# Layer 0: sampling-matrix matmuls issued two groups at a time, window products spread out, and the shared convolution block computed by ScalarE and GpSimd

## The chip, the cores and the metric

The kernel runs on one core of one Trainium2 chip. The metric is device microseconds of one execution of the program. The kernel before was run three times: 3473.86, 3480.29 and 3483.97 us, median 3480.29 us. One more execution was profiled; it took 3483.37 us, of which its trace spans 3481.5 us.

## The reference

Two layers act on x of shape (2, 512, 64, 64), float32. The change touches only layer 0, a deformable convolution with a residual; layer 1 (attention over the pixels, batch norm, residual) takes its result.

```python
# layer 0
x = x + L0(gn(x))                               # gn: group norm, 32 groups
# L0, with C=512, G=16 groups, 9 points, 64x64 pixels:
xproj  = inp @ in_w + in_b                      # 512x512 projection per pixel
x1     = depthwise_conv3x3(x) + dw_b            # 9 taps per channel
x1     = gelu(layernorm(x1) * ln_g + ln_b)
offset = x1 @ off_w + off_b                     # 16*9*2 columns
mask   = softmax((x1 @ mask_w + mask_b) by group)   # 16*9 columns
out    = sum over 9 points of mask * bilinear(xproj at point + offset)
out    = out @ out_w + out_b
```

## The kernel before

A period of layer 0 handles one chunk: 8 rows of 64 pixels, 512 pixels (`CH`), of one image. There are `NSEQ` = 16 chunks, 8 for each of two images. Channels lie in 4 blocks of 128 partitions (`KB`). Offsets are small enough that every sample falls into a 5x5 window around its pixel, so the bilinear gather is turned into a product: for each pixel and group, 25 window weights `aw`, then a matmul of those weights with patches of `xproj`.

Each chunk passes through generators, and every `yield` is a place at which another generator may go on:

- `project(i)`: normalizes the input (`xn`, ScalarE, L782), multiplies by `in_w` (`pq`, L792), copies (`xj`, L798) and stores to DRAM.
- `features(i)`: the depthwise convolution. One tap starts `conv` (L828 on ScalarE for the first three chunks, L830 on GpSimd after that), the other 8 taps in each of 4 blocks are multiply-adds on VectorE (L841), 32 in all. Then the mean over channels (`p_mean`, a matmul with ones, L855), the subtraction (L860), squares (L863), the variance, its root (L872), a reciprocal (L874), a product (L875) and Gelu (L879) into `feat`. For chunks 0 and 1, which fill the pipeline, GpSimd computes one block (`SHARED`) alone in `share`: a product (L821) and an addition (L822) for each of 8 taps.
- `weights(i)`: four tiles of 128 pixels, each four matmuls into `po` (L896) and an addition of the bias into `o` on VectorE (L903); exponent (L910), softmax, ramps `tx`, then nine products on VectorE (L941), of which eight are added into `aw` by GpSimd (L946). Products alternate between two buffers, `o[:, 0]` and `o[:, 1]`. The result is copied in four parts (`at`, ScalarE, L951), transposed by TensorE (`p_tr`, L960) and copied into `awT` (L961).
- `sample(i)`: eight groups of four matmuls `pb` (L989) spread the weights over the patch positions, each group copied by ScalarE into `bt` (L994); then eight groups of eight matmuls `pa` (L1008) with the patches, copied into `dT` (L1019), then four tiles of output `py` (L1028), each followed on VectorE by an addition into `res` (L1033) and statistics (L1034), and a store. `pb` and `pa` share two PSUM buffers (tag `big`); `po`, `py`, `pq`, `p_mean` and `p_tr` share four (tag `mm`).

A `pb` group reads `awT` on partitions `32*t` upward, with `t = c // 2`, c the column of the pixel in its strip of eight. So a group with d0 divisible by 8 uses t = 0 and 1, and the next one t = 2 and 3:

```python
for d0 in range(0, PR * PC, 4):
    for k in (0, 2, 1, 3):
        r, c = divmod(d0 + k, PC)
        off, t = SEL0 - (r * SX + c), c // 2
```

No scheduler reorders anything: `manual_schedule` keeps each engine's instructions in the order in which they are emitted, and `period` (L1058) writes out by hand how seven generators are interleaved: `y` is the sample of the chunk before (its last part), `v` the weights of this chunk, `m` its sample, `w` the weights of the next, `f` the features of the chunk after that, `g` those of a later one, `p` a projection, `more` statistics of the second image. `period` runs for chunks 0 to 13; `next_to_last` and `last_period` for 14 and 15. Before it, L1186 on fills the pipeline. A tile comes free when the last reader of its buffer is done, so a buffer's reuse is a wait on another engine.

Of the kernel before, what the change touches and what calls it, by code (L numbers as in the profile page):

```python
# [10 lines left out]
F32 = mybir.dt.float32  # L11
I32 = mybir.dt.int32
AF = mybir.ActivationFunctionType
ALU = mybir.AluOpType
# [562 lines left out]
def window_path(ctx: ExitStack, tc: tile.TileContext, t_in: dict, out: bass.AP, far: bass.AP, sums: bass.AP):  # L577
# [67 lines left out]
    with ExitStack() as l0:  # L645
# [159 lines left out]
        def features(i):  # L805
# [9 lines left out]
            def share(kb):  # L815

                x = io.tile([P, ROWS + 2, W], F32, name="raw", bufs=3)
                for tap in (0, 2, 3, 4, 5, 6, 7, 8):
                    dst, src, wt = tap_of(kb, tap)
                    part = x[:, :ROWS, : dst.shape[2]]  # L820
                    nc.gpsimd.tensor_scalar(part, src, wt, None, ALU.mult)  # L821
                    nc.gpsimd.tensor_add(dst, dst, part)  # L822

            fill = i < 2
            for kb in BLOCKS if i < 3 else range(KB):
                dst, src, wt = tap_of(kb, 1)
                if i < 3:
                    nc.scalar.activation(dst, src, AF.Identity, bias=dw_b[:, kb : kb + 1], scale=wt)  # L828
                else:
                    nc.gpsimd.tensor_scalar(dst, src, wt, dw_b[:, kb : kb + 1], ALU.mult, ALU.add)  # L830
                if fill and kb == SHARED:
                    share(kb)
                if fill or kb == KB - 1:
                    yield
            tot = None if fill else sm.tile([P, CH], F32, tag="tot", name="tot")
            for kb in BLOCKS if fill else range(KB):
# [23 lines left out]
            nc.vector.tensor_sub(a, a, mu.unsqueeze(1).to_broadcast([P, KB, CH]))  # L860
            f = cv.tile([P, KB, CH], F32, tag="feat", name="feat")
            for kb in range(KB):
# [10 lines left out]
            yield  # L873
            nc.vector.reciprocal(rstd, rstd)  # L874
            nc.vector.tensor_mul(a, a, rstd.unsqueeze(1).to_broadcast([P, KB, CH]))  # L875
            yield

# [9 lines left out]
        def weights(i):  # L887
# [5 lines left out]
            for t in range(4):  # L893
                po = ps.tile([P, CH], F32, tag="mm", name="po")
                for kb in range(KB):
                    nc.tensor.matmul(  # L896
                        po[:, : 3 * GP], f[:, kb, t * P : (t + 1) * P], om_w[:, kb].rearrange("p a k g -> p (a k g)"),
                        start=(kb == 0), stop=(kb == KB - 1),
                    )
                    if kb == 1:  # L900
                        yield
                yield
                nc.vector.tensor_add(  # L903
                    o[:, :, :, t * G : (t + 1) * G].rearrange("p a k g -> p (a k) g"),
                    po[:, : 3 * GP].rearrange("p (a g) -> p a g", g=G), om_b.rearrange("p a k g -> p (a k) g"),
                )
                yield
# [29 lines left out]
            for e, k in enumerate((4, 0, 1, 2, 3, 5, 6, 7, 8)):  # L937
                kx, ky = divmod(k, 3)
                dst = aw[:, ky : ky + 3, kx : kx + 3, :]
                pk = dst if k == 4 else o[:, e % 2].rearrange("p (y x) q -> p y x q", x=3)  # L940
                nc.vector.tensor_mul(  # L941
# [115 lines left out]
        def period(y, v, m, w, f, g, p, more, last, ahead, taps):  # L1057
# [12 lines left out]
            for k, count in enumerate(taps):  # L1070
                for _ in range(2):
                    m()
                    w()
                f(count)
                w()
                if k < 2:
                    more()
# [16 lines left out]
            y(2)  # L1094
            more()
            f()
            y()
            m()
            p()
            for k, steps in enumerate((2, 2, 1, 0)):  # L1100
                p()
                w(steps)
                if k == 0:
# [4 lines left out]
                if k == 2:  # L1108
                    more()
                    w(2)  # L1110
                if k < 3 and (k or not last):
                    m()
                if k == 0:
                    f()
                if k == 2:
                    w(2)
                    g()

        def next_to_last(y, v, m, w):

            v(4)
            y()
            w(12)
            for steps, tiles in ((1, 2), (1, 2), (2, 2), (1, 1)):
# [58 lines left out]
        def more():  # L1183
            next(later, None)

        with tc.manual_schedule():  # L1186
# [25 lines left out]
            p1(4)  # L1212
            f0(3)
            f1(8)
# [3 lines left out]
            p2()  # L1218
            v(3)
            f1()  # L1220
            for _ in range(3):
                more()
            p2(4)
            v(3)
            f()
            v(3)
            f(3)
            v(3)
            f1()
            f(3)  # L1230
            f1()
            v(2)
            p2(2)
            v(3)
            p2(2)
            v(4)
            f1()
            p2(2)
            v(5)
            f1(2)  # L1240
            p2(2)
            more()
            next(products)
            run(output_bias())
            more()
            f(4)
            v(4)
            for i in range(NSEQ):
# [7 lines left out]
                if i + 2 >= NSEQ:  # L1256
                    (next_to_last if i + 1 < NSEQ else last_period)(y, v, m, w)
                    y, v = m, w
                    continue
                ahead, taps = (4, (9, 7, 6, 6)) if i else (0, (4, 6, 6, 6))  # L1260
                period(y, v, m, w, f, g, Chain(project, i + 3), more, i + 3 == NSEQ, ahead, taps)
# [652 lines left out]
```

## Time and profile before

| what | value |
|---|---|
| median of three executions | 3480.29 us |
| the profiled execution | 3483.37 us |
| its span | 3481.5 us |
| layer 0, to the last `py` | about 1290 us |
| a period between 326 and 1144 us | 73.0 to 76.2 us, mean 74.4 |
| TensorE busy, 326 to 1144 us | 772.30 of 818 us |
| VectorE busy, same stretch | 640.54 us |
| ScalarE busy, same stretch | 569.11 us |
| GpSimd busy, same stretch | 345.56 us |
| mean granted TensorE clock | 0.969 |

The trace of one execution names each instruction's start, its length, and what ended the idle time before it. "x16" behind a matmul counts passes: a float32 matmul appears as two, a transpose as one. Busy time of TensorE includes pipelined ends, so a stretch of back-to-back matmuls is read from start to start. "Clock" is the share of full speed that TensorE was granted; it is 1.00 or 0.50 in any moment. Idle time of an engine off the chain costs nothing.

A period's start is taken here as the start of L860, once per period on VectorE: for example 626.88, 701.97 and 777.06 us.

### The profile page before, as it was taken

What the parts mean: (1) busy time and instruction counts of PE and PEld (TensorE: products, weight loads), DVE (VectorE), ACT (ScalarE), POOL (GpSimd) and SP (SyncE); (2) the same over time, 40 slices, a digit from 0 to 9 for tenths busy, and PEclk for the clock granted to TensorE, in tenths of its full rate; (3) what the DMA queues carried; (4) which work ended last, traced back from release to release, by engine and by line L of the source; (5) the groups of instructions that cost most, each with busy time, mean ns of one, the idle gap of its engine ahead of it and who ended that gap; (6) DMA issues with size and microseconds to landing.
All of it is one profiled execution on the core that took longest, in us unless ns stands there. A gap on an engine that the chain in (4) does not pass through costs nothing.

```text
span 3481.5 us, 38488 instructions
## 1 busy us (share of the span) xinstructions
PE 3227.7 (93%) x14171; PEld 2279.8 (65%) x14171; DVE 2666.6 (77%) x3682; ACT 1323.0 (38%) x1799; POOL 751.9 (22%) x674
## 2 busy tenths in 40 slices
PE   5889999999999789899999999999899999999990
PEld 2455555555555467578787787887578787787880
DVE  8788777778778648787696886977787696885875
ACT  2576766667767543211312203113221212202105
POOL 5344443344443310100101001000100101101112
PEclk9999999999999899999999999999999999999995
DMA  6334433223342248966768658656966767758788
GB/s 220 96 99 135 127 121 101 88 88 115 105 127 80 70 136 289 290 188 176 216 186 229 195 169 223 211 180 220 280 195 179 212 194 219 206 162 231 234 294 351
DMA packets 238390, 629.99 MB, mean 181 GB/s; under 512 B 28112, under 2 KB 45136, under 8 KB 237168
## 3 DMA queue, kind: packets, MB, share of 16 engines
q1 hardware_dynamic: 181456, 431.07, 37.9%
q0 software_dynamic: 43936, 159.40, 17.7%
q10 hardware_dynamic: 12800, 36.97, 3.0%
q8 instruction: 114, 1.87, 0.2%
q14 instruction: 84, 0.69, 0.1%
HBM read 410.15 MB, written 124.91 MB: 154 GB/s over the span
## 4 chain that ended last, share of the span: by engine, by line
PE 69%; DVE 14%; POOL 5%; DMA 4%; ACT 4%; issue 3%; SPq 0%; ACTq 0%; POOLq 0%; DVEq 0%
PE accy L1528 22%; PE accx L1528 17%; PE pS L1435 7%; PE py L1028 4%; POOL aw L946 4%; PE po L896 4%; PE pvy L1686 3%; DVE conv L841 3%; PE pb L989 2%; PE pa L1008 2%; PE pvx L1686 2%; PE pq L792 2%; PE pk L1758 1%; DMA wv<-vsum 1%; ACT at L951 1%
## 5 line engine op out<-in xcount | busy, mean ns | idle before, releaser
L1528 PE MATMUL accy<-tt,v 128*128 128x256 f32 x2016 | 601.0, 380 | 0.8 <-DVE ct L1557 0.6
L1440 ACT ACTIVATE e<-pS 128x1024 f32<-128x1024 f32 x256 | 248.3, 1021 | 723.4 <-PE pS L1435 719.2
L1528 PE MATMUL accx<-e,v 128*128 128x256 f32 x1792 | 472.8, 386 | 0.0
L1528 PE MATMUL accy<-e,v 128*128 128x256 f32 x1792 | 461.2, 380 | 0.0
L841 DVE SCALAR_TENSOR_TENSOR conv<-xn,L_conv_dw_w_sb,conv 128x504 f32<-128x504 f32 x496 | 420.5, 855 | 52.3 <-POOL conv L830 37.2
L1528 PEld LDWEIGHTS accy<-tt,v 128*128 128x128 f32 x2016 | 383.3, 190 | 54.9 <-DVE ct L1557 1.0
L1528 PEld LDWEIGHTS accx<-e,v 128*128 128x128 f32 x1792 | 334.6, 191 | 121.8 <-issue 80.7
L1528 PEld LDWEIGHTS accy<-e,v 128*128 128x128 f32 x1792 | 341.2, 190 | 46.6
L1507 DVE TENSOR_TENSOR tt<-e 128x256 f32<-128x256 f32 x448 | 187.8, 419 | 177.2 <-PE accy L1528 148.9
L1508 DVE TENSOR_TENSOR tt<-tt,e 128x512 f32<-128x512 f32 x448 | 310.0, 692 | 15.3
L1528 PE MATMUL accx<-tt,v 128*128 128x256 f32 x1008 | 300.9, 380 | 9.0 <-DVE tt L1507 9.0
L994 ACT COPY bt<-pb 96x1024 f32<-96x1024 f32 x124 | 243.9, 1975 | 162.3 <-PE pb L989 160.8
L1008 PEld LDWEIGHTS pa<-bt,patch 96*128 96x128 f32 x2048 | 247.7, 195 | 61.3 <-issue 31.4
L1435 PE MATMUL pS<-q,keys 64*128 64x512 f32 x1024 | 256.7, 620 | 9.2 <-ACT e L1440 9.2
L1008 PE MATMUL pa<-bt,patch 96*128 96x128 f32 x2048 | 251.9, 279 | 11.7 <-ACT bt L994 11.3
L946 POOL TENSOR_TENSOR aw<-aw,o 128x576 f32<-128x576 f32 x128 | 230.9, 1804 | 121.8 <-DVE o L941 114.2
L1028 PE MATMUL py<-dT,L_conv_out_w_sb 128*128 128x512 f32 x512 | 252.3, 640 | 1.4 <-ACT awT L961 1.4
L1449 POOL DMA_DIRECT2D tot<-e x144 | 124.0, 887 | 588.8 <-DVE e L1425 316.7
L792 PE MATMUL pq<-in_w,xn 128*128 128x512 f32 x512 | 235.1, 602 | 3.6 <-ACT xn L782 3.3
L1453 POOL DMA_DIRECT2D tot<-e x32 | 17.4, 544 | 974.0 <-DVE e L1425 835.8
L1533 ACT COPY u<-accx 128x256 f32<-128x256 f32 x56 | 20.8, 372 | 519.7 <-PE accx L1528 516.9
L896 PE MATMUL po<-om_w_pg,feat 128*128 128x432 f32 x512 | 217.0, 550 | 0.7 <-ACT feat L879 0.7
(245 smaller groups left out, 4721.8 us busy)
## 6 DMA issues: line engine op xcount, KB each, us to landing
v<-wv SPq DMA_DIRECT2D x436, 448.0 KB
tot<-e POOLq DMA_DIRECT2D x176, 512.0 KB, 7.0
patch<-xt SPq DMA_DIRECT2D x256, 192.0 KB
v<-ww SPq DMA_DIRECT2D x56, 448.0 KB
wv<-vform SPq DMA_DIRECT2D x48, 512.0 KB
wv<-vsum SPq DMA_DIRECT2D x48, 384.0 KB
xt<-xj SPq DMA_DIRECT2D x128, 128.0 KB
res<-in_x SPq DMA_DIRECT2D x64, 256.0 KB
```

What stands on the lines that cost most here:

```text
L792: nc.tensor.matmul(pq, xn[:, kb, 1 + 2 * t : 3 + 2 * t, :].rearrange("p r c -> p (r c)"), in_w[:, kb, :], start=(kb == 0), stop=(kb == KB ...
L841: nc.vector.scalar_tensor_tensor(dst, src, wt, dst, ALU.mult, ALU.add)
L896: nc.tensor.matmul(po[:, : 3 * GP], f[:, kb, t * P : (t + 1) * P], om_w[:, kb].rearrange("p a k g -> p (a k g)"), start=(kb == 0), stop=(k ...
L946: nc.gpsimd.tensor_add(dst, dst, pk)
L994: copy(bt[:SN].rearrange("s g q d -> s d (g q)")[:, d0 : d0 + 4, :], pb[:SN])
L1008: nc.tensor.matmul(pa[:, p], xp[:SN, p, cb * P : (cb + 1) * P], bt[:SN, 4 * cb : 4 * cb + 4, PX * s + p, :], start=True, stop=True,)
L1028: nc.tensor.matmul(py, out_w[:, kb, cb * P : (cb + 1) * P], dT[:, kb, :], start=(kb == 0), stop=(kb == KB - 1))
L1435: nc.tensor.matmul(p[:, a, :], keys[r, i, (2 * u + h) * P : (2 * u + h + 1) * P], c.q[r, qh, :], start=True, stop=True,)
L1440: nc.scalar.activation(e.rearrange("p a q -> p (a q)"), p.rearrange("p a q -> p (a q)"), AF.Exp)
L1507: nc.vector.tensor_sub(t[:, 0], x[:, 1], x[:, 3])
L1508: nc.vector.tensor_add(t[:, 1:3], t[:, 0].unsqueeze(1).to_broadcast([P, 2, HQ]), x[:, 0:3:2])
L1528: nc.tensor.matmul(out, v[:, blk, :], op, start=(first and g == 0), stop=(final and g == NG))
```

## The change

`share` puts its products on ScalarE, in two alternating buffers, and keeps the additions on GpSimd; it is emitted after all four first taps. Chunk 1 uses `awT` for its squares. In `weights`, the yield inside a tile's four matmuls is gone, and products use three buffers, `o[:, 2]` being free by then. A yield stands between the reciprocal and the product in `features`. In `period`, two steps of `m` now stand together, followed by one step of `w`, so two `pb` groups and then one whole `po` tile are emitted; 14 taps instead of 4 (8 instead of none in the first period) come ahead of the first output tile, 18 instead of 28 after it; and products stand around the reciprocal and its product. The order of the fill is rewritten.

```diff
             def share(kb):
-                x = io.tile([P, ROWS + 2, W], F32, name="raw", bufs=3)
-                for tap in (0, 2, 3, 4, 5, 6, 7, 8):
+                x = [io.tile([P, ROWS + 2, W], F32, name="raw", bufs=3) for _ in range(2)]
+                for k, tap in enumerate((0, 2, 3, 4, 5, 6, 7, 8)):
                     dst, src, wt = tap_of(kb, tap)
-                    part = x[:, :ROWS, : dst.shape[2]]
-                    nc.gpsimd.tensor_scalar(part, src, wt, None, ALU.mult)
+                    part = x[k % 2][:, :ROWS, : dst.shape[2]]
+                    nc.scalar.activation(part, src, AF.Identity, scale=wt)
                     nc.gpsimd.tensor_add(dst, dst, part)
...
-                if fill and kb == SHARED:
-                    share(kb)
                 if fill or kb == KB - 1:
                     yield
+            if fill:
+                share(SHARED)
...
-            f = cv.tile([P, KB, CH], F32, tag="feat", name="feat")
+            f = awT.rearrange("p g w -> p (g w)").rearrange("p (k c) -> p k c", k=KB)
+            if i != 1:
+                f = cv.tile([P, KB, CH], F32, tag="feat", name="feat")
...
             nc.vector.reciprocal(rstd, rstd)
+            yield
             nc.vector.tensor_mul(a, a, rstd.unsqueeze(1).to_broadcast([P, KB, CH]))
+            if i == 1:
+                f = cv.tile([P, KB, CH], F32, tag="feat", name="feat")
...
-                    if kb == 1:
-                        yield
                 yield
...
-                pk = dst if k == 4 else o[:, e % 2].rearrange("p (y x) q -> p y x q", x=3)
+                pk = dst if k == 4 else o[:, e % 3].rearrange("p (y x) q -> p y x q", x=3)
...
             for k, count in enumerate(taps):
-                for _ in range(2):
-                    m()
-                    w()
+                m(2)
+                w()
                 f(count)
                 w()
...
             more()
+            w(2)
             f()
+            w()
+            f()
+            w(2)
             y()
             m()
             p()
-            for k, steps in enumerate((2, 2, 1, 0)):
+            for k in range(4):
                 p()
-                w(steps)
...
                 if k == 2:
                     more()
-                    w(2)
+                    w()
                 if k < 3 and (k or not last):
                     m()
                 if k == 0:
                     f()
+                if k == 1:
+                    w()
...
             v(4)
             y()
-            w(12)
+            w(8)
...
-            f0(3)
+            f0(4)
             f1(8)
             next(products)
             fetch(0, 0)
             fetch(0, 1)
             p2()
-            v(3)
-            f1()
+            v(4)
             for _ in range(3):
                 more()
+            f1()
+            v(2)
+            f1()
+            v(2)
             p2(4)
-            v(3)
+            v()
+            f1()
+            v()
             f()
             v(3)
...
-                ahead, taps = (4, (9, 7, 6, 6)) if i else (0, (4, 6, 6, 6))
+                ahead, taps = (14, (5, 5, 4, 4)) if i else (8, (5, 5, 4, 4))
```

The rest of the rewritten fill only redistributes the same steps `v`, `f1`, `p2` and `f`. On TensorE the order of a period changes in one place: eight times "four `pb`, two `po`" becomes four times "eight `pb`, four `po`".

More of the change, by code (lines that the diff above doesn't have):

```diff
@@ L1218, in window_path @@
             p2()
-            v(3)
-            f1()
+            v(4)
             for _ in range(3):
                 more()
+            f1()
+            v(2)
+            f1()
+            v(2)
             p2(4)
-            v(3)
-            f()
-            v(3)
[L1227 to L1230, printed above, removed]
+            v()
+            f1()
+            v()
+            f()
+            v(3)
+            p2(4)
+            v(4)
             f1()
             v(2)
-            p2(2)
+            f1(3)
             v(3)
[L1235 to L1242, printed above, removed]
+            p2(4)
             next(products)
             run(output_bias())
-            more()
-            f(4)
+            f(6)
             v(4)
```

## The prediction

> **What bounds the kernel now.** I read the page first, then the chain of waits over layer 0, then one steady period (626.88 to 701.97 us) engine by engine, and at last other places where the operations that the change pairs already stand in pairs. By windows, the period and the two stretches of it that matter:
>
> ```profile
> 626.90:702.00 75.10, 71.35 (x311) 40.07 (x310) 57.77 (x64) 51.71 (x71) 30.94 (x21) 0.95 0.33 102
> 660.00:664.10 4.10, 2.46 (x14) 1.26 (x12) 3.63 (x4) 4.05 (x8) 3.41 (x4) 1.00 0.69 211
> 664.10:670.90 6.80, 6.13 (x12) 2.98 (x12) 0.63 (x1) 2.60 (x6) 1.43 (x1) 0.50 0.65 200
> 671.80:693.80 22.00, 21.59 (x98) 10.03 (x97) 21.25 (x28) 15.87 (x9) 2.99 (x2) 1.00 0.16 57
> ```
>
> Columns are length, then busy time of TensorE, weight loads, VectorE, ScalarE and GpSimd, then clock, DMA share and GB/s. TensorE has work for 71.35 of 75.10 us: its order is the bound, and a period shrinks where TensorE issues less, or waits less. It loses in two places: the transposes (660 to 664, followed by two half-speed windows of 3.4 us), and the 22 us in which `pb` and `po` alternate. Of that stage TensorE's timeline shows:
>
> ```profile
> 671.85 1.11 PE L989 MATMUL pb<-awT,sel 25*96 25x256 f32 x8
> 672.88 1.72 PE L896 MATMUL po<-om_w_pg,feat 128*128 128x432 f32 x4
> 674.53 1.10 PE L989 MATMUL pb<-awT,sel 25*96 25x256 f32 x8
> ...
> 690.63 1.11 PE L989 MATMUL pb<-awT,sel 25*96 25x256 f32 x8
> 691.67 1.72 PE L896 MATMUL po<-om_w_pg,feat 128*128 128x432 f32 x4
> 693.80 3.39 PE L1008 MATMUL pa<-bt,patch 96*128 96x128 f32 x28 [0.41 <-ACT bt L994]
> ```
>
> A unit takes 2.68 us from start to start (671.85 to 674.53): 1.03 for `pb`, 1.65 for `po`. Eight make 21.46; with the wait for the last copy, 21.95 us until `pa`. In the period for chunk 14, which calls two `m` steps together already, the same timeline reads:
>
> ```profile
> 1198.50 1.25 PE L896 MATMUL po<-om_w_pg,feat 128*128 128x432 f32 x3
> 1199.68 1.13 PE L989 MATMUL pb<-awT,sel 25*96 25x256 f32 x16
> 1200.74 3.70 PE L1028 MATMUL py<-dT,L_conv_out_w_sb 128*128 128x512 f32 x8
> 1204.37 1.41 PE L989 MATMUL pb<-awT,sel 25*96 25x256 f32 x16
> ```
>
> Sixteen passes take 1.06 us, as eight do above: the second group is free, because it uses other partitions. This is what the change makes of every `pb` group. VectorE and ScalarE, by their timelines:
>
> ```profile
> 660.36 4.37 DVE L841 SCALAR_TENSOR_TENSOR conv<-xn,L_conv_dw_w_sb,conv 128x504 f32<-128x504 f32 x4 [3.53 <-POOL conv L830]
> 671.95 0.75 DVE L1033 SCALAR_TENSOR_TENSOR res<-py,L_conv_out_b_sb,res 128x512 f32<-128x512 f32 x1 [7.22 <-PE py L1028]
> 659.61 1.61 ACT L951 COPY at<-aw 128x400 f32<-128x400 f32 x2 [0.57 <-POOL aw L946]
> 1177.02 1.56 ACT L951 COPY at<-aw 128x400 f32<-128x400 f32 x2 [3.83 <-POOL aw L946]
> 1200.83 3.79 ACT L994 COPY bt<-pb 96x1024 f32<-96x1024 f32 x2 [17.11 <-PE pb L989]
> 42.97 30.02 DVE L841 SCALAR_TENSOR_TENSOR conv<-xn,L_conv_dw_w_sb,conv 128x512 f32<-128x512 f32 x26
> ```
>
> VectorE idles 7.22 us before the first output tile; the copies that feed the transposes wait only 0.57 us for the products in a steady period, but 3.83 in the one of chunk 14; a pair of `bt` copies takes about 3.8 to 3.9 us.
>
> **What the Trainium skill says.** "TensorE: Matmul & The Clock Gate", Part 3: matmuls in different row groups run concurrently. The trace agrees: 1.06 us for sixteen passes beside 1.03 for eight. The same page, Part 1: after an idle window of about 3.4 us the clock is halved; Part 4: transposes don't count as busy in the same way. The trace agrees: every period from 252 us on has one or two half windows (3.41 or 6.83 us) behind its transposes. "GPSIMD Engine Reference", section 1: its SBUF interfaces are shared with VectorE. The fill agrees: a tap takes 0.74 us alone, 1.05 beside GpSimd's addition and 1.62 beside its product.
>
> **The `pb`/`po` stage, 14 periods.** Count from the first `pb`. A pair of groups takes 1.06. Four `po` in a row are eight passes: the trace has 0.466 between the first two, 0.363 between later ones, 0.455 to the next `pb`, so 0.466 + 6 x 0.363 + 0.455 = 3.10. TensorE alone would cycle in 4.16, four times 16.6. ScalarE needs 8 copies of 1.96 = 15.7 from 1.15 on (673.00 less 671.85), so the two PSUM buffers decide. Copies 1 and 2 end at 3.1 and 5.1. TensorE is back at 4.16 for group 3 (buffer free), but group 4 waits until 5.1; its `po` run to 9.2, while copies 3 and 4 end at 7.3 and 9.2. Groups 5 and 6 start at 9.2 without a wait, `po` to 13.4, copies at 10.4 to 14.3; groups 7 and 8 start at 13.4 and 14.3, `po` to 18.5, copies to 18.5. So `pa` starts at 18.5 instead of 21.95: **3.45 us less**, 14 x 3.45 = 48.3. From below: if the pairs don't overlap here, only half the switches (about 0.4 each, 4 of them) and most of the last wait (0.4) go, 2.0 a period, 28 in all. From above: with no buffer wait 1.15 + 15.7 = 16.9, so 5.0 a period, 70.
>
> **Taps and products.** VectorE's row of a period, from L860 with the trace's durations: 16.0 us to the reciprocal with five products ahead of it instead of three (each 0.68; a third buffer spares the 1.30 us wait for GpSimd), reciprocal 3.4, one product, L875 from 20.0 instead of 18.8. Gelu on ScalarE starts 1.3 later, and behind it, in order, stand a table load, four Gelu, two `xj` and eight `dT` copies, 10.2 us, so `at` comes at 32.6. Before it came at 32.7, released by GpSimd. GpSimd's eight additions now end near 27.2 (11.4 + 8 x 1.97) instead of 32.7, but nobody takes them sooner: **0** a period, hidden behind ScalarE's queue. If the cover fails I bound it at 1.3 either way. Chunk 14 has no projection; there 3.83 - 1.25 = **2.6** are gained, once.
>
> L830 waits for Gelu instead of GpSimd's additions, taps start at 31.9 (before: 33.5). The 32 taps of this period take 27.5 us (rows of 4.37, 6.85, 6.21, 5.40 and 4.64), 0.86 each; 14 of them 12.0, to 43.9. With `res` and statistics 1.4, 18 taps 15.5, four additions into `o` 2.1 and ramps 3.5 it is ready at 66.4. TensorE asks for the mean at 45.0 + 18.5 + 3.7 + 3.4 = 70.6. So 14 taps fill the 7.22 us of idleness and leave 4.2 us of slack; at 43.9 the first `py`, done at 45.0 now, isn't kept waiting. Store and buffer behind it aren't late: the buffer of `py` is next wanted by the fourth `po` tile, 12 us on. Five early periods have 61.5 us of VectorE work instead of 57.8 (statistics of image 2), which eats the slack; I charge 1.0 each, **+5**.
>
> **DMAs.** Each period issues the same transfers. `xj` stores come about 1.3 us later and sixteen patch loads with them; patches land more than 20 us ahead of their `pa`: 0.
>
> **The fill.** Before, GpSimd makes 8 products (1.85) and 8 additions (1.47) for each of two chunks; 26 taps of VectorE take 30.0 us beside it. After, additions alone, one in 1.55 us: 12.5 us with taps at 1.05 and the rest at 0.78, so 12 + 14 taps = 23.5 us, 6 less. ScalarE pays: a 512-wide activation with weights per partition costs about 0.7 by L828, but two buffers tie it to GpSimd, 8 x 1.4 = 11 us, twice. Behind the second stand the `xj` copies and squares of chunk 0, which begin at 78.9 now and would at 79 to 81. So what VectorE gains is lost there again, and `po` comes 0 to 3 us later, while weights of chunk 0 have shorter work left. Bounds -6 and +6; I take **-1**.
>
> **The sum.** -48.3 - 2.6 + 5 - 1 = -46.9, on 3483.4 of the profiled execution: 3436.5. The transposes keep their idle time (first, second, third and fourth group released at 33.5, 34.7, 36.9, 38.0 by the copies, as against 33.7, 34.4, 36.6, 37.9), so half windows stay at 1.3 a period, 1.7 us each; but where the free-running window falls is open: -12 to +15. The median lies 3.1 below the profiled execution; 3480.3 less 46.9 gives **3433**. Layer 1, 2175 us of the span, isn't touched, and starts that much earlier.
>
> **Rivals.**
> 1. The pairs don't overlap, or overlap but the copies hold TensorE up: 28 of the 48 remain, with the rest 3450 to 3463. Against it: the 1.06 us above; for it, only eight such pairs exist, none with `po` behind it. 0.15.
> 2. Half windows become rarer, since periods are no longer near 22.0 windows (75.09 us) but near 20.5: 12 to 20 us more, 3412 to 3418. 0.08.
> 3. The edit does nothing: TensorE waits for ScalarE as before. Eight copies of 1.96 without a gap are 15.7 of 21.95 us, so copies alone can't hold it. 3470 to 3490. 0.03.
> 4. Slower: VectorE becomes the bound, because taps slow down beside other engines. Ready at 66.4 with 0.86 a tap, it reaches today's 75.1 with 8.7/32 = 0.27 more: from 1.13 a tap on the kernel is slower, which is just what the fill shows (29.3/26). At 1.2, 2.3 us a period, 3515. Against it: that was beside GpSimd's products; beside the steady taps GpSimd has only first taps, a memset and three additions. 0.05.
>
> **How the numbers follow.** The forecast, 0.69, has its own range 3418 to 3447. About 0.3%, 10 us, is what a measurement of this kernel can tell from no change. Forecast, rivals 1 and 2 are faster: 0.92; rival 3 is the same, 0.03; rival 4 slower, 0.05. The range 3412 to 3462 holds forecast, rival 2 and nearly all of rival 1.
>
> **What would show it.** Right: `pb` in rows of x16 of 1.1 to 2 us; `bt` copies in pairs, `pa` 18 to 19 us after the first `pb`; periods of 69.5 to 71.5 us; VectorE's wait for `py` gone; GpSimd's last addition into `aw` 5 us before `at`. Wrong: a new wait of `pb` for `bt` over 1.5 us a cycle; L860 waiting for taps; a mean clock under 0.95 in periods; L860 of chunk 1 later than 116 us (now 110.8).

## The result, and the profile after

The changed kernel takes 3461.33 us (median of five executions, 3457.41 to 3463.31); beside it the kernel before takes 3477.49 (3473.86 to 3483.97). The ratio is 0.9951, 95% interval 0.9936 to 0.9965: 17 us faster, where 46.9 were forecast. The profiled execution took 3457.41 us (span 3455.6) and was the shortest of its five, while the profiled one of before, at 3483.37, lies near the top of its own; the two traces are therefore 26 us apart, 10 more than the medians.

The stage in which `pb` and `po` alternate went as forecast. TensorE's timeline of the changed kernel, from the first `pb` of a steady period:

```profile
733.40 1.13 PE L992 MATMUL pb<-awT,sel 25*96 25x256 f32 x16
734.46 3.17 PE L901 MATMUL po<-om_w_pg,feat 128*128 128x432 f32 x8
737.56 1.88 PE L992 MATMUL pb<-awT,sel 25*96 25x256 f32 x16
...
746.70 1.84 PE L992 MATMUL pb<-awT,sel 25*96 25x256 f32 x16
748.47 3.17 PE L901 MATMUL po<-om_w_pg,feat 128*128 128x432 f32 x8
751.73 3.84 PE L1011 MATMUL pa<-bt,patch 96*128 96x128 f32 x32
```

Four cycles, and `pa` 18.33 us after the first `pb` (before: 21.95; forecast: 18.5). The second and fourth pair take 1.88 and 1.84 instead of 1.13, the waits of 0.7 for a free buffer that the working had put at 0.9. Between 688 and 1118 us the period is 71.7 us, where the kernel before has 73.7 between 702 and 1144. The gain in the stage is 3.6 us, that in the period only 2.0. By windows, one period, and the stretch in which it transposes, in three periods (columns: length, busy time of TensorE, weight loads, VectorE, ScalarE and GpSimd, clock, DMA share, GB/s):

```profile
688.20:760.00 71.80, 66.73 (x311) 39.11 (x310) 60.68 (x64) 51.14 (x71) 32.35 (x21) 0.98 0.34 107
...
726.60:730.00 3.40, 2.66 (x9) 1.96 (x10) 3.29 (x5) 3.38 (x7) 1.43 (x1) 0.55 0.59 187
798.30:801.70 3.40, 2.65 (x9) 1.96 (x10) 3.29 (x5) 3.38 (x7) 1.43 (x1) 0.55 0.59 190
870.00:873.40 3.40, 2.70 (x9) 1.96 (x10) 3.29 (x5) 3.38 (x7) 1.43 (x1) 0.55 0.58 187
```

From 688 us on every period has exactly one window at half clock, 3.41 us long and always about 38.8 us after its L860, behind the transposes; the last three rows begin 38.4 us after it. TensorE idles 5.1 us of 71.8, so it is something ahead of it that is late. What TensorE waits for shows in the costliest groups of the page: for `pa`, 24.4 us of idle time in the whole kernel, 17.0 of them ended by a copy into `dT`, where before there were 11.7, ended by `bt`:

```profile
L1011 PE MATMUL pa<-bt,patch 96*128 96x128 f32 x2048 | 253.8, 280 | 24.4 <-ACT dT L1022 17.0
```

The timelines of VectorE, ScalarE and TensorE in the same period lead back from there:

```profile
698.66 3.42 DVE L944 TENSOR_TENSOR o<-my,tx 128x576 f32<-128x576 f32 x3
...
703.39 2.62 DVE L944 TENSOR_TENSOR o<-my,tx 128x576 f32<-128x576 f32 x2
705.93 3.34 DVE L876 RECIPROCAL rstd<-rstd 128x512 f32<-128x512 f32 x1
709.20 0.69 DVE L944 TENSOR_TENSOR o<-my,tx 128x576 f32<-128x576 f32 x1
709.81 2.27 DVE L878 TENSOR_TENSOR conv<-conv,rstd 128x2048 f32<-128x2048 f32 x1
```

```profile
712.16 1.28 ACT L884 ACT_TABLE_LOAD   x1 [7.16 <-DVE conv L878]
...
721.06 1.48 ACT L1022 COPY dT<-pa 32x256 f32<-32x256 f32 x4
722.57 0.90 ACT L954 COPY at<-aw 128x400 f32<-128x400 f32 x1
```

```profile
718.06 2.05 PE L1011 MATMUL pa<-bt,patch 96*128 96x128 f32 x16 [1.43 <-ACT dT L1022]
```

The rows of VectorE merge products of different length. Of the five ahead of the reciprocal, three take 0.74 to 0.87 us and two take 1.96, each beside an addition that GpSimd had begun. Here is the first of these two, then the same product in the kernel before, where it waits for its buffer instead:

```profile
699.61 1.85 POOL L949 TENSOR_TENSOR aw<-aw,o 128x576 f32<-128x576 f32 x1 [0.69 <-DVE o L944]
700.12 1.96 DVE L944 TENSOR_TENSOR o<-my,tx 128x576 f32<-128x576 f32 x1
```

```profile
640.21 0.76 DVE L941 TENSOR_TENSOR o<-my,tx 128x576 f32<-128x576 f32 x1 [1.30 <-POOL aw L946]
```

The reciprocal is at 17.7 after L860 (forecast 16.0), L878, the product that was L875, at 21.6 (forecast 20.0, before 18.8). ScalarE waits 7.16 us for it, and behind Gelu on ScalarE stand the `dT` copies for which `pa` waits, and `at`, 34.4 us after L860 (forecast 32.6, before 32.7).

### The profile page after: what moved, and what is told of

Same layout as the page of the kernel before. It is cut to its first block, busy times and chain, and to the rows that moved or that the text cites. A ratio compares the mean times of both kernels' runs of the same rounds, so it can differ in the third digit from the quotient of the medians.

```text
span 3455.6 us, 38512 instructions
## 1 busy us (share of the span) xinstructions
PE 3182.6 (92%) x14171; PEld 2271.1 (66%) x14171; DVE 2713.1 (79%) x3682; ACT 1326.1 (38%) x1815; POOL 731.1 (21%) x658
## 4 chain that ended last, share of the span: by engine, by line
PE 67%; DVE 14%; ACT 9%; DMA 6%; issue 3%; POOL 1%; SPq 0%; ACTq 0%; POOLq 0%; DVEq 0%
PE accy L1530 22%; PE accx L1530 17%; PE pS L1437 6%; PE po L901 4%; PE py L1031 4%; PE pvy L1688 3%; DVE o L944 3%; PE pa L1011 2%; PE pvx L1688 2%; PE pb L992 2%; ACT feat L884 2%; ACT dT L1022 2%; DVE rstd L876 1%; PE pk L1760 1%; ACT at L954 1%
## 5 line engine op out<-in xcount | busy, mean ns | idle before, releaser
L997 ACT COPY bt<-pb 96x1024 f32<-96x1024 f32 x124 | 234.7, 2005 | 115.6 <-PE pb L992 107.9
L1011 PE MATMUL pa<-bt,patch 96*128 96x128 f32 x2048 | 253.8, 280 | 24.4 <-ACT dT L1022 17.0
L949 POOL TENSOR_TENSOR aw<-aw,o 128x576 f32<-128x576 f32 x128 | 241.4, 1886 | 61.9 <-DVE o L944 55.8
L1031 PE MATMUL py<-dT,L_conv_out_w_sb 128*128 128x512 f32 x512 | 242.2, 618 | 0.1
L1530 PEld LDWEIGHTS accx<-tt,v 128*128 128x128 f32 x1008 | 191.6, 190 | 33.6 <-DVE tt L1509 7.5
```

The costliest lines, as they stand in the source:

```text
L949: nc.gpsimd.tensor_add(dst, dst, pk)
L997: copy(bt[:SN].rearrange("s g q d -> s d (g q)")[:, d0 : d0 + 4, :], pb[:SN])
L1011: nc.tensor.matmul(pa[:, p], xp[:SN, p, cb * P : (cb + 1) * P], bt[:SN, 4 * cb : 4 * cb + 4, PX * s + p, :], start=True, stop=True,)
L1031: nc.tensor.matmul(py, out_w[:, kb, cb * P : (cb + 1) * P], dT[:, kb, :], start=(kb == 0), stop=(kb == KB - 1))
L1530: nc.tensor.matmul(out, v[:, blk, :], op, start=(first and g == 0), stop=(final and g == NG))
```

## Experiments

Beside each time below stands its ratio to the kernel before, measured in the same series on the same chip, with its 95% interval; 0.001 is 3.5 us. The changed kernel is at 0.9951.

### Pairs: alone, with the taps, and taken out of the change

Pairs alone, in the kernel before:

```diff
             for k, count in enumerate(taps):
-                for _ in range(2):
-                    m()
-                    w()
+                m(2)
+                w(2)
                 f(count)
```

> The kernel before with one edit: two steps of m, then two of w, in each of the four cycles of taps, so that pb groups come in pairs. Taps, products and fill stay as before. Theory A (the pairs free TensorE, but taps bind once TensorE is faster): 28 taps of 0.86 us are 24 us of VectorE in a stage of 18.3 us, so L860 comes where it came before and with it Gelu and the window weights; 3465 to 3482 us, periods of 73.5 to 74.5 us. Rival B (the stage's 3.45 us a period count by themselves): about 3432 us. Rival C (the stage's gain is given back by whatever TensorE waits for next, in any arrangement of the taps): no more than 3460 to 3480 here and in the next kernel too.

Measured: 3473.22 us, 0.9979 (0.9972 to 0.9986). Theory A holds in the time, though most periods from the eighth on take 72.0 us, less than the 73.5 to 74.5 it gave. VectorE, which has 28 taps left in the stage, is now the last to arrive: in the period from 701 us TensorE waits 1.8 us for the sum of the taps before it can form the mean.

The pairs, and with them the taps ahead of the first output tile as in the change, but nothing else of it:

```diff
-                ahead, taps = (4, (9, 7, 6, 6)) if i else (0, (4, 6, 6, 6))
+                ahead, taps = (14, (5, 5, 4, 4)) if i else (4, (5, 5, 4, 4))
```

> The kernel before with two edits: the pairs, and 14 taps ahead of the first output tile instead of 4 (4 instead of none in the first period), with (5, 5, 4, 4) in the cycles. Products, their two buffers and the fill stay as before. Theory A (what the change lost, it lost by the spread of the products, which slows them beside GpSimd's additions and moves Gelu and the dT copies late): the stage's 14 times 3.45 us arrive, less 5 in the early periods; about 3433 us, 3425 to 3442, periods of 71 us or less, product L875 18.8 us or less after L860. Rival B (the loss was in the fill alone): 4 or 5 us below the changed kernel, about 3456. Rival C (the gain of the stage is given back whatever the products do): 3457 to 3465.

Measured: 3425.52 us, 0.9840 (0.9823 to 0.9856), steady periods of 69.6. L875 at 18.75 us after L860, as before. Rivals B and C fall: two edits of a few lines bring three times what the whole change brings. How the two edits go together shows in what VectorE waited for ahead of L860 (its one line in each kernel, first the pairs alone, then with the taps):

```profile
L860 DVE TENSOR_TENSOR conv<-conv,p_mean x16: 2277/2280/2283, 72.8 to 1134.8; 128x2048 f32<-128x2048 f32 x16
...
its engine sat idle before it (us, times) until:
```

```profile
L860 DVE TENSOR_TENSOR conv<-conv,p_mean x16: 2278/2287/2289, 72.9 to 1086.5; 128x2048 f32<-128x2048 f32 x16
...
its engine sat idle before it (us, times) until:
  PE p_mean L855: 23.5, 13
```

With pairs alone nothing stands under "until": VectorE never waits for the mean, as it never does in the kernel before. With the taps it waits for TensorE's mean 13 times, 23.5 us in all. The taps moved into VectorE's idle time ahead of `py` are what lets the pairs count.

The counterpart, the changed kernel without its pairs:

```diff
+                    if kb == 1 and 1 <= i < NSEQ - 1:
+                        yield
...
-                m(2)
-                w()
+                for _ in range(2):
+                    m()
+                    w()
```

> The changed kernel with the pairs undone: the yield within a po tile is back for chunks 1 to 14, and the steps of m and w alternate again. Taps ahead, spread products, three buffers and the new fill stay. Theory A (the pairs bring 3.45 us a period by themselves): 14 times 3.45 more than the changed kernel, about 3509 us, so slower than before. Rival B (the period is bound by VectorE's chain, so that TensorE's stage has slack): within 10 us of the changed kernel, 3455 to 3470. Rival C (the pairs gain half): about 3485 us.

Measured: 3512.58 us, 1.0093 (1.0076 to 1.0109), so 49 us more than the changed kernel by the ratios, 51 by the medians. Theory A holds within 3 us. The stage's gain is whole in the changed kernel; something else takes most of it away.

### Products: order, neighbours, third buffer

The changed kernel with the products where they were:

```diff
-            w(2)
-            f()
-            w()
-            f()
-            w(2)
+            f(2)
             y()
...
-            for k in range(4):
+            for k, steps in enumerate((2, 2, 1, 0)):
                 p()
+                w(steps)
...
                     more()
-                    w()
+                    w(2)
...
-                if k == 1:
-                    w()
```

> The changed kernel with the products put back where they were: none between reciprocal and product, the steps (2, 2, 1, 0) and 2 behind them. Pairs, taps ahead, three buffers and the new fill stay. Theory A (products beside GpSimd's additions delay the chain Gelu, dT, pa by 1.7 us a period): 14 times 1.7 is 24 us less than the changed kernel, about 3437 us, 3430 to 3447; products of about 0.7 us; pa's wait for dT back near 12 us in all. Rival B (the loss was in the fill): within 4 us of the changed kernel, 3457 to 3465. Rival C (the order of the products is right and the old one makes the end of the window weights late): slower than the changed kernel, up to 3480.

Measured: 3418.54 us, 0.9818 (0.9802 to 0.9834), 43 us below the changed kernel by the medians and 46 by the ratios. Theory A has the sign and the place, but its 24 us was too little, and one detail was wrong: products are not about 0.7 us. VectorE's timeline of this kernel, from the first product on:

```profile
677.69 3.42 DVE L944 TENSOR_TENSOR o<-my,tx 128x576 f32<-128x576 f32 x3
681.03 0.74 DVE L1036 SCALAR_TENSOR_TENSOR res<-py,L_conv_out_b_sb,res 128x512 f32<-128x512 f32 x1
681.80 0.69 DVE L1037 BATCH_NORM_STATS2 stats<-res 128x6 f32<-128x512 f32 x1
682.41 3.33 DVE L876 RECIPROCAL rstd<-rstd 128x512 f32<-128x512 f32 x1
685.78 2.29 DVE L878 TENSOR_TENSOR conv<-conv,rstd 128x2048 f32<-128x2048 f32 x1
...
689.38 7.06 DVE L944 TENSOR_TENSOR o<-my,tx 128x576 f32<-128x576 f32 x5
```

Products are as slow here, up to 2 us, but five of them stand behind L878, where only the additions and the copies `at` follow on them, and these come at 32.0 us, earlier than in the changed kernel. L878 comes at 18.6, and `pa` waits 8.4 us in all, for `bt` again. Averages over the seven periods from the eighth L860 on, in us after L860:

| | L878 / L875 | first `at` | first transposes | last transposes | first `pb` | period |
|---|---|---|---|---|---|---|
| before | 18.76 | 32.72 | 33.66 | 38.54 | 44.09 | 74.2 |
| changed | 21.62 | 34.38 | 35.32 | 40.95 | 45.21 | 71.7 |
| products gathered | 18.57 | 32.01 | 33.73 | 37.66 | 41.57 | 68.1 |
| without additions (below) | 19.19 | 31.94 | 33.70 | 38.25 | 42.44 | 69.0 |

Order costs 3.6 us a period: 1.6 at the first transposes, which stand on TensorE behind the `pa` that waited 1.43 us for `dT`, and another 1.7 by the last ones, where the copies `at` lie further apart and TensorE is slow. The windows of the gathered kernel at the same distance from L860 show the second:

```profile
705.60:709.00 3.40, 3.40 (x16) 1.42 (x18) 3.26 (x6) 0.73 (x2) 0.00 (x0) 1.00 0.64 218
773.50:776.90 3.40, 3.40 (x6) 1.29 (x6) 3.27 (x5) 0.71 (x2) 0.00 (x0) 0.68 0.65 216
841.40:844.80 3.40, 3.13 (x10) 1.67 (x11) 3.26 (x6) 2.18 (x5) 1.17 (x1) 1.00 0.49 175
```

The clock is 1.00 in two of three; a half window reaches into the middle one. Sampled every 0.85 us over six periods, the gathered kernel has two half-clock windows, the changed one six. A period of the gathered kernel with such a window is 69.4 us, without it 67.9; so one costs 1.5, and four of six make 1.0 us a period of the 3.6.

Position or neighbours? The changed kernel without GpSimd's additions, all else in its place:

```diff
-                if k != 4:
-                    nc.gpsimd.tensor_add(dst, dst, pk)
                 yield
```

> The changed kernel without GpSimd's additions of the products into aw (eight per chunk), so window weights hold one product of nine only; pairs, taps, the order of the products and the fill stay, and VectorE still makes all nine products. Theory A (the products are slow because GpSimd's additions run beside them): products of 0.68 to 0.76 us in place of 1.1 to 1.3; L878 at about 19 us after L860 instead of 21.6, pa's wait for dT nearly gone, 3420 to 3430 us. Rival B (three more products ahead of L878 cost this wherever the additions are, by their number alone): L878 at 20.5 to 21 and 3445 to 3460. Rival C (the additions' end is what holds the copies at, and so the period): 3420 or less, but with products still over 1 us.

Measured: 3424.28 us, 0.9844 (0.9819 to 0.9869). L878 at 19.2. All products of the run (min/median/max in ns), first of the changed kernel, then without additions:

```profile
L944 DVE TENSOR_TENSOR o<-my,tx x128: 686/868/1968, 129.9 to 1199.8; 128x576 f32<-128x576 f32 x128
```

```profile
L944 DVE TENSOR_TENSOR o<-my,tx x128: 684/749/874, 130.8 to 1154.9; 128x576 f32<-128x576 f32 x128
```

None is over 0.88 us now. The copies `at` had 5 us to spare behind the additions in the changed kernel, so leaving these out can't act through their end. Nor does it act through the taps: VectorE still waits for the mean, 44.5 us in all for 46.0. Theory A is shown: with the products ahead of L878 but undisturbed, 37 of the 43 us are back (37 of 46 by the ratios). The other 6 to 9 are left for their number and position, as far as two series can tell. Rival B is out by 20 us, and rival C by the length of the products. In the gathered kernel half of the products are slow:

```profile
L944 DVE TENSOR_TENSOR o<-my,tx x128: 689/1950/1982, 130.7 to 1159.5; 128x576 f32<-128x576 f32 x128
```

The median of 1.95 us is about 0.68 for the product and 1.30 for the rest of an addition, as long as VectorE waited for one in the kernel before: with three buffers a product that meets an addition waits for its end. "SBUF — State Buffer" of the Trainium skill, section "SBUF: two separate sides", says that too: a port pair shared by VectorE and GpSimd, held exclusively for a whole instruction, which a VectorE instruction with two SBUF inputs needs against a GpSimd one that reads SBUF. Product and addition are such a pair, and the trace agrees.

The third buffer, in the kernel with pairs and taps:

```diff
-                pk = dst if k == 4 else o[:, e % 2].rearrange("p (y x) q -> p y x q", x=3)
+                pk = dst if k == 4 else o[:, e % 3].rearrange("p (y x) q -> p y x q", x=3)
```

> The kernel before with pairs, 14 taps ahead and the third product buffer; fill and products' order as before. Against the kernel with pairs and taps alone (3425.5) it shows the third buffer, against the one with the products gathered (3418.5) the fill. Theory A (new fill +4 us, and the rest of what lies between those two is the third buffer, about 11 us): about 3414. Rival B (the third buffer only turns waits for a buffer into slower products and brings nothing; the new fill is a gain of 7): about 3425.

Measured: 3413.58 us, 0.9807 (0.9781 to 0.9834), and 3408.27, 0.9792 (0.9772 to 0.9812), when run once more with the kernels of the next part. The third buffer brings 12 to 17 us, so rival B is out by the time. The first half of its mechanism is there, though: the products that waited 1.30 us for a buffer take 1.95 us instead of 0.76. What is left as a gain is that the additions behind L875 follow each other every 1.88 us instead of 2.06, so that `at` comes 0.7 us earlier (32.01 for 32.71). The period falls by twice that, from 69.6 to 68.1; half-clock windows, which stand in five of the last six steady periods with two buffers and in one or two with three, are at 1.5 us each about as much again.

### The fill

Against 0.9792 to 0.9807 with the old fill, 0.9818 with the new one looks like a cost, of 4 to 9 us. The first suspect was ScalarE, whose products for chunk 1's shared block stand ahead of chunk 0's squares. In the gathered kernel:

```diff
-                    nc.scalar.activation(part, src, AF.Identity, scale=wt)
+                    if i == 0:
+                        nc.scalar.activation(part, src, AF.Identity, scale=wt)
+                    else:
+                        nc.gpsimd.tensor_scalar(part, src, wt, None, ALU.mult)
```

> The kernel with the products gathered again, in which the shared block of chunk 1 has its products on GpSimd as before; ScalarE makes only those of chunk 0. Theory A (in the changed fill chunk 0's squares stand on ScalarE behind the eight products of chunk 1's share, each of which waits for a GpSimd addition, so the reciprocal L876 of chunk 0 comes at 90.3 instead of 84.6): squares about 5 us earlier, L860 of chunk 1 at 109 to 111 instead of 115, about 5 us off the time, 3412 to 3415. Rival B (the fill is bound elsewhere, by the order of the taps and of po): no change, 3417 to 3420. Rival C (GpSimd's products slow VectorE's taps as much as they free ScalarE): within 2 us.

Measured: 3418.67 us, 0.9824 (0.9798 to 0.9850): no change. L860 of chunk 1 stays at 114.7. Theory A fell, and the profile of this kernel says why. Its ScalarE timeline:

```profile
83.11 1.23 ACT L798 COPY xj<-pq 128x512 f32<-128x512 f32 x2 [14.03 <-DMA wvfc<-wc_part]
84.23 2.19 ACT L868 ACTIVATE feat<-conv 128x512 f32<-128x512 f32 x4
90.81 0.69 ACT L877 ACTIVATE rstd<-p_mean,eps 128x512 f32<-128x512 f32 x1 [4.39 <-PE p_mean L858]
```

(These lines are from its second run.) With ScalarE's products gone, chunk 1's first `xj` copy waits 14 us for a store: `wc_part`, the weight products of `value_weights`, uses the buffers of `xj`. The kernel before has the same wait in the same place, only shorter:

```profile
77.05 0.58 ACT L798 COPY xj<-pq 128x512 f32<-128x512 f32 x1 [8.10 <-DMA wvfc<-wc_part]
```

SyncE's queue in the kernel before and in the changed one:

```profile
44.45 11.43 SPq L800 DMA_DIRECT2D xt<-xj  x8
55.97 0.48 SPq L717 DMA_DIRECT2D xt<-raw  x1
...
71.94 2.72 SPq L1166 DMA_DIRECT2D wvfc<-wc_part  x2
```

```profile
45.19 16.33 SPq L800 DMA_DIRECT2D xt<-xj  x8
61.61 0.48 SPq L717 DMA_DIRECT2D xt<-raw  x1
...
76.63 1.90 SPq L1173 DMA_DIRECT2D wvfc<-wc_part  x2
```

In the new fill three of chunk 0's four `xj` copies stand on ScalarE behind chunk 0's shared products, most of which wait for a GpSimd addition. So the stores of `xj` end 5.6 us later, the sixteen border stores (L717, L718) begin as much later, and the store of `wc_part` behind them 4.7. The border isn't needed that soon, so it can go behind `wc_part`. Four kernels on one chip: both fills, each with and without this edit; the first and third are kernels already shown, run once more.

```diff
-            border()
             more()
             p1()
             for kb in range(KB):
                 p1()
                 f1()
                 if kb == 1:
                     next(products)
                     next(products)
+            border()
```

> The kernel with the products gathered and chunk 1's shared products on GpSimd once more, on the chip of the next three runs. 3416 to 3420; against the next kernel it shows the border stores, against the one after it the two fills: theory A (the new fill costs 3 to 5 us, since chunk 0's xj copies stand on ScalarE behind products that wait for GpSimd, so that SyncE's border stores and the store of wc_part behind them go out 5 us late) says 3 to 5 above the old fill; rival B (no difference) within 1.5.

> As the run before, with the sixteen border stores emitted behind chunk 1's first steps, so behind the two stores of wc_part in SyncE's queue. Theory A: wc_part lands 10 us earlier, chunk 1's xj copies and chunk 0's squares no longer wait for it; squares at 76 to 78 us instead of 83.6, L860 of chunk 1 at 108 to 110 instead of 114.7, 4 to 6 us less than the run before. Rival B (squares wait next for something else, or L860 of chunk 2 does not follow): within 1.5 us of the run before.

> The kernel before with pairs, 14 taps ahead and the third buffer once more. About 3413.5, 3 to 5 us below the mixed fill by theory A, the same by rival B.

> The old fill with the border stores behind the stores of wc_part. Theory A: squares at 74 to 77 instead of 79 to 81, 2 to 4 us less than the run before, about 3410. Rival B: VectorE's taps beside GpSimd's products hold the reciprocal at 84 to 85 us anyway, within 1.5 us.

| fill | border first | border behind `wc_part` |
|---|---|---|
| new (chunk 1's products on GpSimd) | 3419.17, 0.9816 (0.9797 to 0.9836) | 3407.01, 0.9791 (0.9773 to 0.9810) |
| old | 3408.27, 0.9792 (0.9772 to 0.9812) | 3408.75, 0.9793 (0.9775 to 0.9811) |

The new fill costs 11 us by the medians and 8 by the ratios, more than theory A had; the first pair of these kernels on one chip (3418.67 and 3413.58) had 5 and 6. Moving the border stores takes 12 away (9 by the ratios), twice what theory A gave; with the old fill it brings nothing, as rival B had it. ScalarE's timeline of the new fill with the border behind:

```profile
68.95 0.58 ACT L798 COPY xj<-pq 128x512 f32<-128x512 f32 x1 [0.43 <-PE pq L792]
72.38 0.58 ACT L798 COPY xj<-pq 128x512 f32<-128x512 f32 x1 [2.85 <-PE pq L792]
72.86 2.19 ACT L868 ACTIVATE feat<-conv 128x512 f32<-128x512 f32 x4
77.29 0.69 ACT L877 ACTIVATE rstd<-p_mean,eps 128x512 f32<-128x512 f32 x1 [2.24 <-PE p_mean L858]
```

The squares start 11.4 us earlier (72.86 for 84.23), L860 of chunk 1 at 105.4 for 115.4: the wait for the store is shown to be the cause in this kernel. In the old fill `xj` waits 6.17 us for `pq` instead and the squares stay at 80.0. At 3407.01 us this kernel beats both kernels of the case; the old fill with pairs, taps and third buffer, at 3408.27, can't be told from it.

### The fill in the changed kernel

There, ScalarE's products for chunk 1 end at 80.1 us and the store lands at 81.2, so two things hold the squares. The two edits shown above, applied to the changed kernel: the border stores alone, and then chunk 1's products on GpSimd as well.

> The changed kernel, products spread as in the change, with the border stores emitted behind chunk 1's first steps. Theory A (two things hold chunk 0's squares in the changed fill: wc_part's store until 81.2 us, and chunk 1's eight ScalarE products, which wait for GpSimd's additions until 80.1; taking one away leaves the other): squares at about 81 instead of 82.3, 1 to 3 us less than the changed kernel, 3458 to 3461. Rival B (the store alone holds the fill here too): 10 to 12 us less, about 3449.

Measured: 3457.39 us, 0.9921 (0.9901 to 0.9942); squares at 80.3, L860 of chunk 1 at 111.1 instead of 114.2. That is near theory A, and so are the 4 us less by the medians. By the ratios it is 10 us, which is what rival B gave, so the time doesn't tell the two apart. In its trace the 3 us at chunk 1 have shrunk to 0.6 by the last L860.

> As the run before, and chunk 1's shared products back on GpSimd. Theory A: both holds are gone, squares at about 73 instead of 82.3, L860 of chunk 1 near 105, 10 to 12 us less than the changed kernel: about 3449. Rival B (the steady periods of the changed kernel, bound by the chain through the products, take the gain of the fill back): within 3 us of the changed kernel.

Measured: 3451.37 us, 0.9901 (0.9880 to 0.9922); squares at 74.8, L860 of chunk 1 at 105.1. Ten us below the changed kernel by the medians, as theory A has it; by the ratios it is 17, with an interval of some 10. So both holds are real: the squares moved by 2.1 us with the first edit and by 5.4 more with the second. Its trace, though, taken from the longest of its six executions, keeps 9.1 us at chunk 1 and only 2.9 at the last L860: the five periods from its eighth L860 on are 72.3 to 73.8 us, where the changed kernel has 71.7. The chain that rival B names is not longer there: L878 and `at` stand 21.6 and 34.4 us after L860, as in the changed kernel. What differs is the half clock behind the transposes, which lasts 6.8 us instead of 3.4 in two of these periods and comes up to 2.0 us later in the others. How much of a head start survives such windows stays open within these limits.

## Why the prediction was wrong

The sign was right and 3461 lies in the range, but the gain was 17 us and not 47. In the order of its sum, with the ratios turned into us of 3480:

| step | forecast | measured | by |
|---|---|---|---|
| stage, with the taps that make room for it | -48.3 | -56 in the kernel before, -49 in the changed one | pairs and taps, pairs undone |
| third buffer | in "products" | -12 to -17 | third buffer added |
| products' order | 0 | +46 (43 by the medians) | products gathered |
| chunk 14 | -2.6 | about -0.8 | traces |
| five early periods | +5 | not separated | |
| fill | -1 | +5 to +11 | both fills |

Stage, third buffer, fill and order make -56 - 14 + 8 + 46 = -16, beside -17 measured. The kernels form one chain from the kernel before to the changed one, so this says only that the series fit each other.

**The pb/po stage, 14 periods:** right, down to the waits for a buffer in the second and fourth pair, 18.33 us for 18.5. Rival 1 (pairs don't overlap) and rival 3 are out.

**Taps and products** is the step that failed, in one clause: "each 0.68; a third buffer spares the 1.30 us wait for GpSimd". The third buffer does away with the wait, and by doing so puts the next product beside the running addition, where it takes about 1.95 us. The price of 0.68 was that of products with no addition running beside them. From there the error runs on by the prediction's own chain: L878 at 21.6 instead of 20.0, Gelu later by as much, `at` at 34.4 instead of 32.6. The slow products cost more than these differences show. The reciprocal came at 15.4 us before; two more products of 0.68 and 1.30 less of waiting make 15.5, not the 16.0 of the working, so at 17.7 it is 2.3 late.

Its conclusion, "hidden behind ScalarE's queue", had no room: the working put `at` at 32.6, a tenth of a us ahead of before, so whatever L878, the head of that queue, loses beyond that is paid in full. It also followed that queue to `at` alone. The `dT` copies stand in it too, `pa` waits 1.43 us for them in the period shown, and the transposes come behind `pa`.

The right price stood in the fill of the kernel before. The prediction read there that a tap, which has two inputs in SBUF like a product, takes 1.05 us beside GpSimd's addition and 1.62 beside its product. The trace has it the other way round; L822 is the addition, L821 the product:

```profile
48.07 1.48 POOL L822 TENSOR_TENSOR conv<-conv,raw 128x504 f32<-128x504 f32 x1
48.47 1.63 DVE L841 SCALAR_TENSOR_TENSOR conv<-xn,L_conv_dw_w_sb,conv 128x512 f32<-128x512 f32 x1
49.65 1.88 POOL L821 TENSOR_SCALAR raw<-xn,L_conv_dw_w_sb 128x512 f32<-128x512 f32 x1
50.13 1.05 DVE L841 SCALAR_TENSOR_TENSOR conv<-xn,L_conv_dw_w_sb,conv 128x504 f32<-128x504 f32 x1
```

The tap that meets the addition ends 0.55 us behind it; the product shown from the changed kernel ends 0.62 us behind its own. In the changed fill, where GpSimd has additions alone, eight taps in a row take 1.62 to 1.73 us, not the 1.05 of the working. The tap beside GpSimd's product ends before that product does, so for that pair the trace doesn't show the hold for a whole instruction that the page on SBUF states; GpSimd's spans are rough in a profile.

The bound, "1.3 either way" if the cover fails, was too tight: 3.6 a period. It left out the slowed products and the half windows; the text held these at 1.3 a period, because the transposes' releases were to stay where they are, and they moved by 1.7. **Chunk 14** gained 0.8 instead of 2.6, read from the last L860 to the last `py` of layer 0 (146.4 to 145.6); without additions it gained 3.3, so it is the same term: `at` is no longer released by GpSimd there but by Gelu.

What it said of VectorE's taps in the steady periods was right: its wait for `py` fell from 7.22 to 0.26 us, it waits 4.1 us for the mean (forecast 4.2), 14 taps take 11.79 us (12.0). GpSimd's last addition ends 5 us before `at`, as foretold. Rival 4, slower taps, did not occur in the periods; the slowing came at another instruction. The prediction cited the shared interface, and applied it to the taps alone.

**The fill:** L860 of chunk 1 came at 114.2, short of the 116 that was to mean a failure, and the fill still cost 5 to 11 us. The working saw the squares begin "at 79 to 81" behind ScalarE's products; they began at 82.3. It took their start of 78.9 in the kernel before as given, where the trace shows 8.10 us of waiting for a store just ahead of it. It put DMAs at 0 for each period and never followed them through the fill, where that store, moved by 4.7 us, held the copies in front of the squares through a buffer that two tiles share. **Half windows**, which the prediction left at -12 to +15, came out rarer where the transposes came early (two in six periods) and fixed at one a period in the changed kernel. Rival 2 had looked for rarer ones at a period near 20.5 windows; the period came to 21.0. In the kernel before these windows stand behind the transposes from 326 us on, not from 252 as the prediction has it: the one in the period before that begins at 261 us, behind 2.05 us in which TensorE waits for the sum of the squares.

## What to carry to other kernels

A duration taken from a trace holds for the neighbours it had there, and which neighbour it had is read from the times of both engines. When a change removes the wait between two engines, price the instruction again with the other engine running beside it, above all a VectorE instruction with two SBUF inputs beside GpSimd. When instructions are moved ahead of one that heads another engine's queue, their new time is paid on that queue as far as it has no slack, so put them behind it. A moved step carries its stores: follow each queue to the next tile that shares a buffer with what it stores.

## What the runs showed that was not expected

- A product of 128x576 float32 takes 0.68 to 0.87 us alone and up to 1.98 beside GpSimd's additions; in the kernel with the products gathered, where half of them meet an addition, the median is 1.95.
- Half-clock windows lock onto the period: at 71.7 us, 21.0 windows of 3.41 us, one falls on the same place behind the transposes in every period from 688 us on; at 67.9 us most periods have none. With the border stores moved in the changed kernel, the window lies 40.4 us after L860 in the period from 614 us and then moves to 38.7, while the period settles from 72.5 to 71.7. About 1.0 of the 3.6 us that the order costs in a period is due to these windows.
- A start 9 to 10 us earlier in the fill may survive whole (3407 for 3419) or be partly given back before the periods settle.
